# Keys of the first pair first, projection by halves, and a last image on two chains: a vision-transformer layer with a scheduling program inside

## The chip, the cores and the metric

The kernel runs on one core of one Trainium2 chip. The metric is the device time of one execution in microseconds (us), lower is better. All times below are of the kernel before the change.

## The reference, cut to what matters

Sixteen images of 3 x 512 x 512 are cut into 16 x 16 patches (1024 tokens of 768 numbers each), and pass a tokenizer and one layer of attention and feed-forward, all in float32:

```
h = patches(x) @ W.T + b                                  # 1024 tokens x 256 per image
q, k, v = split(layernorm(h) @ w_qkv)                     # 8 heads of 32
k = sum_{f=1..256} kan_a[f]*sin(f*k) + kan_b[f]*cos(f*k)  # elementwise on the keys
h = h + softmax(q k^T / sqrt(32)) v @ w_out + b_out
y = layernorm(h)
h = h + shared_mlp(y) + sum over the best 2 of 4 experts of weight_e * expert_e(y)
```

The sum over 256 frequencies for each key element (the "KAN" step) costs as much as the attention. The shared network has layers 256-256-128-256, each expert 256-128-64-256; the gate is a softmax over 4 experts, the best two are weighted by a second softmax.

## The kernel before, in words

**The work.** For an image, the 256 key rows are four "pairs" of heads. The KAN step works in groups `g` of eight key rows, eight groups a pair, 32 an image. A group has three tiles of 128 x 1024 integers: two "slow" waves, loaded from DRAM with copies along the partitions (`load_waves`, L871, tiles `w`), and one "fast" wave that VectorE spreads from a small source tile (`load_source` L890, `spread_waves` L911, tile `f`). GpSimd multiplies each by its frequency (`turn_waves`, L926), ScalarE takes the sine (`sine`, L936), TensorE mixes the two slow waves with the coefficients in tiles of 64 x 32 of the array (`mix`, L960), VectorE multiplies by the fast wave (`times_fast`, L974) and TensorE sums in tiles of 128 x 32 (`add_up`, L993). The finished keys of a pair go to DRAM and back in the order in which the scores need them (`finish_keys` L1012, `stack_keys` L1022). Attention runs once for each pair and each half of the queries, 128 times in all: scores (`score`, L1058, whole array), exponential on ScalarE (`exponential`, L1073), weighting of the values (`weigh`, L1090, tiles of 128 x 64), and a division (`normalize`, L1116 to L1135).

**Rounds.** The program is laid out in 130 rounds (at its end, `for rd in range(B * RI + 2)`). Round `rd` holds four KAN groups and attention number `att = rd - 2`: the first two rounds have no attention, the last two no KAN. On TensorE a round is a *KAN stretch* (four `mix`, then the first half of the sum) and then an *attention stretch* (eight score blocks, the second half of the sum, eight weightings). ScalarE takes the twelve sines of a round, then its eight exponentials, with a table switch before each kind.

**Pieces.** Everything else is put between as "pieces", written as Python generators that yield the engine that they need next and for how long: tokens (`tokens`), layer norms (`first_norm`, `transposed_layernorm`, tiles `hn`, `lnT`, `hnT`, `hT`), `keys`, `queries`, `values`, the projection (`project`), the gate (`gates`, `gate_weights`), and the feed-forward networks (`networks`). They are strung on four chains: 0 has keys, queries and values, 1 has projection, gates and networks, 2 the gate weights, 3 tokens and first norms. A chain goes on in its own order. Two PSUM banks (`side0`, `side1`) serve all pieces.

**What sets the order.** `run` is a planner that runs while the program is built. It keeps a clock for each engine, from costs written in the code, and lays down at each step the instruction that can start first: an item of a fixed queue (`put`, with a cost and dependencies), or the next piece of a chain. For TensorE it weighs a change of tiling (`SWITCH`, `retile`, `together`), and how much a chain is owed: each fixed TensorE item adds `pace * cost` to a chain's `due`, up to `most`, by the table `PACES` (one pair for each chain, L57); a laid piece takes its duration off again (L316), counted by `now["stream"]`, the streamed columns at `PER_COLUMN`. What the planner lays is the order that each engine then executes. Its clock is no measurement; engines wait for each other on the chip with semaphores.

**Places that the change touches.** `keys(b, rows)` makes 128 of the 256 key rows in two blocks of 512 tokens: two products (L263), about 4.2 us of range reduction on VectorE (L531 to L542), an addition on GpSimd (L544), and two stores to the DRAM tile `ud` from SP's queue (L546). The KAN groups of pairs 0 and 1 read rows 0 to 127 (`rows_of`: both blocks). At the start chain 1 holds `first_norm(0, 0), keys(0, 1)` and chain 0 `first_norm(0, 1), keys(0, 0)`. `project(b)` waits for the image's last attention (its "norm") and then does both halves of the tokens. `gates` and `networks` hold named locks (`gates`, `networks`, `s1`, `bands`), since their tiles exist once; for the very last half they run on chain 0 rather than 1, and keep the transposed norm in a part of `hnT`. The row `w5` of weights and the tiles `s1`, `s2`, `e1`, `e2` are shared by all halves.

Of the kernel before, what the change touches and what calls it, by code (L numbers as in the profile page):

```python
# [11 lines left out]
FP = mybir.dt.float32  # L12
# [6 lines left out]
P = 128  # L19
E = 256  # L20
NPAIR = 4
# [34 lines left out]
LAG, LANDS, TABLE, PER_COLUMN, SWITCH, IDLE = 0.06, 2.0, 1.28, 1.0 / 600, 0.18, 0.3  # L56
PACES = ((0.17, 2), (0.48, 3), (0, 0), (0.18, 2))  # L57

# [3 lines left out]
def plain_path(ctx: ExitStack, tc: tile.TileContext, a: dict, out: bass.AP, verdict: bass.AP):  # L62
# [140 lines left out]
    hnT = const.tile([P, 2, N], FP, tag="hnT", name="hnT")  # L203
    hT = const.tile([P, 2, 512], FP, tag="hT", name="hT")

    w5 = const.tile([NW5, 512], FPR, tag="w5", name="w5")
    bands = const.tile([P, 4, 4, NE + 1], FPR, tag="bands", name="bands")
# [13 lines left out]
    ]  # L221
    now = {"chain": 0, "stream": 0, "table": None, "dma": 0.0, "tiling": None}
    free = [0.0, 0.0]
# [63 lines left out]
    def step(c):  # L287

        ch = chains[c]
        now["chain"] = c  # L290
        bank, ch["bank"] = ch["bank"], None
        need = ch["need"]
        before = now["stream"]
        on = need[0] if isinstance(need, tuple) and need[0] in clock else None
        if on:
            at = max(clock[on], ch["ready"] + LAG)
            if on == PE:
                at = max(at, banks(c)[0][0] + LAG)
            ch["ready"] = clock[on] = at + (need[1] or 0.0)
            if bank is not None:  # L300
                free[bank] = ch["ready"]
        elif isinstance(need, tuple):
            ch["ready"] = max(ch["ready"], done[need])
        while True:
            if ch["gen"] is None:
                if not ch["gens"]:
                    ch["need"] = None
                    break
                ch["gen"] = ch["gens"].pop(0)
            try:  # L310
                ch["need"] = next(ch["gen"])
                break
            except StopIteration:
                ch["gen"] = None
        if on == PE:
            took = PER_COLUMN * (now["stream"] - before) + retile(None)  # L316
            ch["due"] -= took
            ch["ready"] = clock[PE] = at + took
# [117 lines left out]

    def transposed_layernorm(h, dst):

        yield from hold("s1")
        st = smp.tile([P, 4, 6], FP, tag="st", name="st")  # L440
# [11 lines left out]
        nc.gpsimd.tensor_tensor(less, less, rstd, ALU.mult)  # L452
        hn = ffp.tile([P, 4, E], FP, tag="s1", name="hn")
        for t in range(4):
# [5 lines left out]
        for c in range(2):  # L460
# [5 lines left out]
            nc.scalar.copy(dst[:, c, :], ps)  # L466
        locks.remove("s1")

# [37 lines left out]

    def keys(b, rows):

# [4 lines left out]
        if "ud" not in st:  # L513
            st["ud"] = udp.tile([E, 2, 2, N], INT, tag="ud", name="ud")
        for blk in range(2):
            yield "hnT", b, blk
# [164 lines left out]

    def project(b):

        yield "norm", 2 * NPAIR * (b + 1) - 1
        st = images[b]
        for half in range(2):
            h = st["h", half]
            for pr in range(2):
                yield GO
                ps = side_tile("proj").rearrange("p (t e) -> p t e", e=E)  # L690
                for t in range(2):
                    for c in range(2):
                        matmul(
                            out=ps[:, t, :],
                            lhsT=aT[:, c, ts(4 * half + 2 * pr + t, P)],
                            rhs=wo[:, c, :],
                            start=(c == 0),
                            stop=(c == 1),
                        )
                yield DVE, 0.63  # L700
                hh = h[:, ds(2 * pr, 2), :]
                nc.vector.tensor_add(hh, ps, hh)
            mark("projected", b, half)

    def gates(b, half, hT):
        yield "projected", b, half
        yield from hold("gates")
        yield from transposed_layernorm(images[b]["h", half], hT)
        yield GO
        ps = side_tile("gate")[:, 0:P]  # L710
        for c in range(2):
            for t in range(4):
# [6 lines left out]
                )  # L719
        now["stream"] += 3 * P  # L720
        yield ACT, 0.25
# [16 lines left out]

    def networks(b, half, hT):

        yield from hold("networks")

# [12 lines left out]
        def first_of_expert(e):  # L755
            yield GO
            ps = hidden(lambda c: w1e[:, 2 * e + c, :], "e1p")
            yield ACT, 0.6
            e1 = ff2.tile([P, 512], FP, tag="e1", name="e1")
            nc.scalar.activation(e1, ps, AF.Relu, bias=b1e[:, e : e + 1])  # L760
            return e1

        def second_of_experts(u, e1):
            yield GO
            ps = side_tile("e2p")
            for s in range(2):
                matmul(
                    out=ps[ts(s, 64), :],
                    lhsT=w2e[:, 2 * u + s, :],
                    rhs=e1[s],  # L770
                    start=True,
                    stop=True,
                )
            yield ACT, 0.6
            t = ff2.tile([P, 512], FP, tag="e2", name="e2")
            nc.scalar.activation(t, ps, AF.Relu, bias=b2e[:, u : u + 1])
            return t

        def weigh_experts(u, t):
            yield GO  # L780
            wb = side_tile("wb")
            matmul(out=wb, lhsT=sel[:, u, :], rhs=w5, start=True, stop=True)
            yield DVE, 0.63
            nc.vector.tensor_mul(t, wb, t)  # L784

        yield from hold("s1")
        s1 = ffp.tile([P, 2, 512], FP, tag="s1", name="s1")
        for m in range(2):
# [7 lines left out]
        for c in range(2):  # L796
# [6 lines left out]
            )  # L803
        locks.remove("s1")
        yield ACT, 0.6
        s2 = ffp.tile([P, 512], FP, tag="s2", name="s2")
        nc.scalar.activation(s2, ps, AF.Relu, bias=b2s)
# [40 lines left out]
        done["written", b, half] = sent(1.6, 0.5)  # L848
        locks.remove("networks")

# [27 lines left out]
    def load_source(p):  # L878
# [21 lines left out]

        deps = rows_of(8 * p) + ([("spread", 8 * p - 1)] if p > 0 else [])
        for j in range(2):
# [203 lines left out]
    def normalize(att):  # L1106
# [14 lines left out]
        def divide(s):  # L1121
# [8 lines left out]
            if i == 0 and b > 0:  # L1130
                deps.append(("projected", b - 1, 1))
            put(DVE, "norm", 0.69, deps, ("divide", att, s), action)
# [829 lines left out]
```

## Time and profile before

| what | value |
|---|---|
| median of 3 runs | 4232.87 us (4228.08 to 4237.59) |
| the profiled execution, own time | 4243.32 us |
| its span in the profile | 4241.8 us |
| PE, busy | 4058.3 us (96%) |
| ACT, busy | 3290.4 us (78%) |
| POOL, busy | 3195.6 us (75%) |
| DVE, busy | 2837.9 us (67%) |
| mean granted TensorE clock | 0.987 |
| moved by DMA | 914.27 MB, mean 216 GB/s |

The profiled execution took 4243.32 us, 10.45 us more than the median of the runs; its span is 1.5 us shorter than its own time. In the profile PE is TensorE, PEld its weight loads, ACT ScalarE, DVE VectorE, POOL GpSimd, SP the engine that issues most DMAs. A line such as `sT<-q,k` says that tile `sT` was written from `q` and `k`; "x4" that four instructions are merged; a bracket at the end is the idle time of the engine before it and what ended that. A float32 product on TensorE appears as two instructions. "Busy" of PE is not full use: an instruction that has started and waits for data counts.

### The profile page before, as it was taken

To read this page: it belongs to the slowest core of one execution; us is meant where nothing else is said; L and a number is where in the kernel's file an instruction comes from. 1 tells how busy PE (TensorE), PEld (TensorE's weight loads), DVE (VectorE), ACT (ScalarE), POOL (GpSimd) and SP (SyncE) were. 2 spreads that over 40 slices of the span, in tenths; PEclk is the share of its full clock that TensorE was granted. 3 is DMA by queue.
4 is the path that set the end of the run, shared out by engine and by line. 5 is a ranking of instruction groups with operands and counts; after the bars stand their busy time and mean duration, and the time that the engine had idled before them with its cause. 6 is when DMAs were issued, how large, how long until landed. Compare 5 with 4: busy or idle time off the path is not lost.

```text
span 4241.8 us, 67578 instructions
## 1 busy us (share of the span) xinstructions
PE 4058.3 (96%) x22753; PEld 1784.1 (42%) x22753; DVE 2837.9 (67%) x4172; ACT 3290.4 (78%) x3939; POOL 3195.6 (75%) x2323
## 2 busy tenths in 40 slices
PE   6889999999999999999999999999999999999997
PEld 4324344444444434444444444444444444443334
DVE  3666766767676675766767767676766767667652
ACT  1587888878888787887878878887888878788782
POOL 2888877787787787787778777877787778787750
PEclk9899999999999999999999999999999999999999
DMA  6988877878878887777878778787887978878750
GB/s 196 257 223 224 230 215 209 247 219 224 234 211 223 224 242 193 230 220 213 245 203 239 210 193 251 215 252 203 233 232 207 256 207 213 240 204 242 189 138 16
DMA packets 587479, 914.27 MB, mean 216 GB/s; under 512 B 58828, under 2 KB 177524, under 8 KB 587124
## 3 DMA queue, kind: packets, MB, share of 16 engines
q1 hardware_dynamic: 580880, 906.98, 77.8%
q8 instruction: 184, 3.01, 0.3%
q10 hardware_dynamic: 6244, 2.88, 0.3%
q14 instruction: 171, 1.40, 0.1%
HBM read 758.64 MB, written 150.99 MB: 214 GB/s over the span
## 4 chain that ended last, share of the span: by engine, by line
PE 59%; ACT 14%; DVE 8%; DMA 8%; issue 4%; SPq 3%; POOL 2%; ACTq 0%; DVEq 0%; POOLq 0%
PE av L1090 15%; PE sT L1058 10%; PE kan L960 6%; ACT w L936 6%; PE tok L263 5%; PE red L993 4%; PE e3p L263 4%; PE e1p L263 3%; ACT f L936 3%; DMA w<-ud 3%; DVE f L974 2%; PE k L263 2%; DMA q<-qd 2%; PE s1p L263 2%; PE proj L263 2%
## 5 line engine op out<-in xcount | busy, mean ns | idle before, releaser
L926 POOL TENSOR_TENSOR w<-w,lane 128x1024 int32<-128x1024 int32 x1024 | 1926.2, 1897 | 533.5 <-DMA w<-ud 289.1
L1073 ACT ACTIVATE es<-sT 128x1024 f32<-128x1024 f32 x1024 | 1033.5, 1023 | 583.0 <-PE av L1090 293.1
L926 POOL TENSOR_TENSOR f<-f,lane 128x1024 int32<-128x1024 int32 x512 | 971.0, 1896 | 193.5 <-DVE f L911 140.0
L936 ACT ACTIVATE w<-w 128x1024 f32<-128x1024 int32 x1024 | 1018.9, 1050 | 37.6 <-POOL w L926 36.2
L1090 PE MATMUL av<-es,v 128*64 128x512 f32 x4096 | 972.2, 605 | 2.3 <-ACT es L1073 2.1
L1116 DVE RECIPROCAL rc<-av 128x256 f32<-128x256 f32 x256 | 434.4, 1731 | 664.2 <-PE av L1090 664.1
L974 DVE TENSOR_TENSOR f<-kan,f 128x1024 f32<-128x1024 f32 x512 | 607.1, 1218 | 208.7 <-ACT f L936 161.6
L1058 PE MATMUL sT<-q,k 128*128 128x512 f32 x2048 | 686.8, 448 | 60.0 <-DVE f L974 26.9
L960 PE MATMUL kan<-w,coef 64*32 64x512 f32 x8192 | 641.4, 603 | 50.4 <-ACT w L936 42.4
L911 DVE STREAM_SHUFFLE f<-src 128x1024 int32<-128x1024 int32 x512 | 673.9, 1354 | 0.7
L1058 PEld LDWEIGHTS sT<-q,k 128*128 128x128 f32 x2048 | 351.7, 190 | 419.1 <-issue 179.3
L936 ACT ACTIVATE f<-f 128x1024 f32<-128x1024 int32 x512 | 512.9, 1052 | 0.0
L1090 PEld LDWEIGHTS av<-es,v 128*64 128x64 f32 x4096 | 260.5, 137 | 568.9 <-issue 499.8
L263 PE MATMUL tok<-wt,x 128*128 128x256 f32 x1536 | 366.9, 390 | 19.6 <-DMA w1s<-in_sW 13.4
L263 PEld LDWEIGHTS tok<-wt,x 128*128 128x128 f32 x1536 | 293.6, 194 | 108.7 <-issue 37.6
L960 PEld LDWEIGHTS kan<-w,coef 64*32 64x32 f32 x8192 | 135.3, 105 | 425.3 <-ACT w L936 248.1
L993 PE MATMUL red<-f,pack 128*32 128x512 f32 x2048 | 272.3, 604 | 0.0
L263 PE MATMUL e1p<-hT,w1e 128*128 128x512 f32 x496 | 242.0, 610 | 4.2 <-DVE e L784 3.8
L457 ACT ACTIVATE hn<-h,less,rstd 128x256 f32<-128x256 f32 x256 | 140.8, 592 | 81.4 <-POOL less L452 81.4
L1123 DVE TENSOR_TENSOR aT<-av,rc 32x512 f32<-32x512 f32 x256 | 176.1, 688 | 6.4
L936 ACT ACT_TABLE_LOAD x128 | 164.2, 1283 | 6.7 <-DMA w<-ud 4.4
L1200 ACT ACT_TABLE_LOAD x128 | 164.2, 1283 | 2.1
(125 smaller groups left out, 3742.2 us busy)
## 6 DMA issues: line engine op xcount, KB each, us to landing
w<-ud SPq DMA_DIRECT2D x2048, 256.0 KB
q<-qd SPq DMA_DIRECT2D x512, 128.0 KB
k<-kd SPq DMA_DIRECT2D x128, 512.0 KB
x<-in_xT SPq DMA_DIRECT2D x128, 384.0 KB
ud<-u SPq DMA_DIRECT2D x64, 512.0 KB
ud<-ui SPq DMA_DIRECT2D x64, 512.0 KB
src<-ud SPq DMA_DIRECT2D x512, 64.0 KB
qd<-qhi SPq DMA_DIRECT2D x64, 256.0 KB
```

Source lines behind the costliest of these rows:

```text
L263: nc.tensor.matmul(out=out, lhsT=lhsT, rhs=rhs, start=start, stop=stop)
L911: nc.vector.stream_shuffle(w, sources[g // 8].rearrange("p r n -> p (r n)"), [4 * (g % 8) + i // 8 for i in range(32)],)
L926: nc.gpsimd.tensor_tensor(w, w, f.to_broadcast([P, N]), ALU.mult)
L936: nc.scalar.activation(x, w, AF.Sin, scale=TURN * 2.0**-32)
L960: nc.tensor.matmul(out=ps[ds(64 * j + 32 * blk, 32), ts(r, 512)], lhsT=coef[ts(r, 64)].rearrange("p e f j -> p (e f j)"), rhs=w[ts(r, 64), ...
L974: nc.vector.tensor_mul(w, kan.pop(g), w)
L993: nc.tensor.matmul(out=rows_of_pair[p][ts(2 * i + r, 32), :], lhsT=pack[:, ds(PACK0 - 16 * (k % 2) - 2 * (k // 2), 32)], rhs=prod[:, ts(r, ...
L1058: nc.tensor.matmul(out=ps[:, ts(s, 512)], lhsT=k4[:, 2 * s + kc // 4, ts(kc % 4, P)], rhs=q4[:, s, :], start=True, stop=True,)
L1073: nc.scalar.activation(es, scores.pop(kc), AF.Exp, scale=SCALE)
L1090: nc.tensor.matmul(out=acc[0][ts(s, 64), :], lhsT=v[:, kc, p % NPAIR, ds(HD * s, 64)], rhs=es[:, ts(s, 512)], start=(kc == 0), stop=(kc == ...
L1116: nc.vector.reciprocal(rc[0][:, part], acc[0][:, part])
L1123: nc.vector.tensor_mul(aT[ds(64 * (i % 2) + HD * s, HD), i // 2, ts(qb, 512)], acc[0][ds(96 * s, HD), :], rc[0][ds(HD + HD * s, HD), :],)
```

## The change

- **Keys of the first pair's rows first.** `keys` takes the blocks to do. Chain 1 does block 0 of rows 0 to 127 after its norm, chain 0 block 1 after its own; only then chain 0 does rows 128 to 255. The first source tile waits until the first two wave tiles have been issued.
- **Projection by half.** `project(b, half)` waits for the last attention of its half only. The division of the next image's first attention waits for the projection of the same half, not of the second. Every half is followed on its chain as before by the gates and networks.
- **Last image.** Its half 0 stays on chain 1, its half 1 (projection, gates, networks) goes to chain 0. Both keep the transposed norm in their own half of `hnT`, take all working tiles from the pool of the wave tiles (`late_tile`, tag `w`, eight buffers), take `w5` from the pool of `f` tiles, and don't use the locks `s1` and `networks`. They wait until the last wave tile has been loaded. The lock `gates` stays.
- **Durations and shares.** `PACES` changes for three chains. A piece may name its tiling (`now["piece"]`), so that the gate counts like the sums and the experts' second layer like the weighting of the values; the gate counts 2P columns rather than 3P, the second layer 512 fewer, the weights' product 300 fewer.

No arithmetic is changed. The diff, cut to its core:

```
-PACES = ((0.17, 2), (0.48, 3), (0, 0), (0.18, 2))
+PACES = ((0.155, 2), (0.44, 2), (0, 0), (0.178, 2.6))
...
         if on == PE:
-            took = PER_COLUMN * (now["stream"] - before) + retile(None)
+            took = PER_COLUMN * (now["stream"] - before) + retile(now["piece"])
+            now["piece"] = None
...
-    def transposed_layernorm(h, dst):
+    def transposed_layernorm(h, dst, late=False):
...
-        yield from hold("s1")
+        if not late:
+            yield from hold("s1")
...
-        hn = ffp.tile([P, 4, E], FP, tag="s1", name="hn")
+        if late:
+            hn = late_tile(N, "hn").rearrange("p (t e) -> p t e", e=E)
+        else:
+            hn = ffp.tile([P, 4, E], FP, tag="s1", name="hn")
...
-    def keys(b, rows):
+    def keys(b, rows, blks=(0, 1)):
...
-        for blk in range(2):
+        for blk in blks:
...
-    def project(b):
+    def project(b, half):
...
-        yield "norm", 2 * NPAIR * (b + 1) - 1
-        st = images[b]
-        for half in range(2):
-            h = st["h", half]
+        yield "norm", 2 * NPAIR * (b + 1) - 2 + half
+        h = images[b]["h", half]
...
+    def late_tile(n, name):
+        return wp.tile([P, N], FP, tag="w", name=name)[:, 0:n]
...
-    def gates(b, half, hT):
+    def gates(b, half, late=False):
         yield "projected", b, half
+        if late:
+            yield "load", total - 1, 1
+            hT = images[b]["hT", half] = hnT[:, :, ts(half, 512)]
+        else:
+            hT = images[b]["hT", half] = hT_
         yield from hold("gates")
...
-        now["stream"] += 3 * P
+        now["stream"] += 2 * P
+        now["piece"] = TILINGS["red"]
...
+        w5 = fp.tile([P, 1024], FPR, tag="f", name="w5")[0:NW5, 0:512] if late else w5_
+        def room(pool, n, name):
+            return late_tile(n, name) if late else pool.tile([P, n], FP, tag=name[:2], name=name)
...
             ps = side_tile("e2p")
+            now["piece"] = TILINGS["av"]
+            now["stream"] -= 512
...
             wb = side_tile("wb")
+            now["stream"] -= 300
...
-        deps = rows_of(8 * p) + ([("spread", 8 * p - 1)] if p > 0 else [])
+        deps = rows_of(8 * p) + [("spread", 8 * p - 1) if p > 0 else ("load", 0, 1)]
...
-                deps.append(("projected", b - 1, 1))
+                deps.append(("projected", b - 1, qb))
...
-    feed(1, first_norm(0, 0), keys(0, 1))
+    feed(1, first_norm(0, 0), keys(0, 0, [0]))
+    feed(0, first_norm(0, 1), keys(0, 0, [1]))
     for b in range(B):
-        feed(0, *([first_norm(0, 1), keys(0, 0)] if b == 0 else [keys(b, 0), keys(b, 1)]))
+        feed(0, *([keys(b, 0)] if b else []), keys(b, 1))
...
-        feed(1, project(b))
+        late = b == B - 1
         for half in range(2):
-            late = half and b == B - 1
-            dst = hnT[:, :, 0:512] if late else hT
-            feed(1 - late, gates(b, half, dst), networks(b, half, dst))
+            feed(1 - (late and half), project(b, half))
+            if late:
+                feed(1 - half, gates(b, half, True), networks(b, half, True))
+        for half in range(2):
+            if not late:
+                feed(1, gates(b, half), networks(b, half))
```

The order of instructions that the planner lays can be read from the built programs without running them; the prediction uses such counts.

More of the change, by code (lines that the diff above doesn't have):

```diff
@@ L203, in plain_path @@
     hnT = const.tile([P, 2, N], FP, tag="hnT", name="hnT")
-    hT = const.tile([P, 2, 512], FP, tag="hT", name="hT")
-    w5 = const.tile([NW5, 512], FPR, tag="w5", name="w5")
+    hT_ = const.tile([P, 2, 512], FP, tag="hT", name="hT")
+    w5_ = const.tile([NW5, 512], FPR, tag="w5", name="w5")
     bands = const.tile([P, 4, 4, NE + 1], FPR, tag="bands", name="bands")
@@ L221, in plain_path @@
     ]
-    now = {"chain": 0, "stream": 0, "table": None, "dma": 0.0, "tiling": None}
+    now = {"chain": 0, "stream": 0, "table": None, "dma": 0.0, "tiling": None, "piece": None}
     free = [0.0, 0.0]
@@ L466, in transposed_layernorm @@
             nc.scalar.copy(dst[:, c, :], ps)
-        locks.remove("s1")
+        if not late:
+            locks.remove("s1")
     def tokens(b, half):
@@ L680, in gate_weights @@
         locks.remove("bands")
-    def project(b):
-        yield "norm", 2 * NPAIR * (b + 1) - 1
-        st = images[b]
-        for half in range(2):
-            h = st["h", half]
[L688 to L703, printed above, removed]
-    def gates(b, half, hT):
-        yield "projected", b, half
+    def project(b, half):
+        yield "norm", 2 * NPAIR * (b + 1) - 2 + half
+        h = images[b]["h", half]
+        for pr in range(2):
+            yield GO
+            ps = side_tile("proj").rearrange("p (t e) -> p t e", e=E)
+            for t in range(2):
+                for c in range(2):
+                    matmul(
+                        out=ps[:, t, :],
+                        lhsT=aT[:, c, ts(4 * half + 2 * pr + t, P)],
+                        rhs=wo[:, c, :],
+                        start=(c == 0),
+                        stop=(c == 1),
+                    )
+            yield DVE, 0.63
+            hh = h[:, ds(2 * pr, 2), :]
+            nc.vector.tensor_add(hh, ps, hh)
+        mark("projected", b, half)
+    def late_tile(n, name):
+        return wp.tile([P, N], FP, tag="w", name=name)[:, 0:n]
+    def gates(b, half, late=False):
+        yield "projected", b, half
+        if late:
[3 more added lines that the diff above has]
+            hT = images[b]["hT", half] = hT_
         yield from hold("gates")
-        yield from transposed_layernorm(images[b]["h", half], hT)
+        yield from transposed_layernorm(images[b]["h", half], hT, late)
         yield GO
@@ L737, in rest, with networks @@
         yield from gen
-    def networks(b, half, hT):
-        yield from hold("networks")
+    def networks(b, half, late=False):
+        if not late:
+            yield from hold("networks")
+        hT = images[b]["hT", half]
+        w5 = fp.tile([P, 1024], FPR, tag="f", name="w5")[0:NW5, 0:512] if late else w5_
+        def room(pool, n, name):
+            return late_tile(n, name) if late else pool.tile([P, n], FP, tag=name[:2], name=name)
         def hidden(lhsT, name):
@@ L758, in first_of_expert @@
             yield ACT, 0.6
-            e1 = ff2.tile([P, 512], FP, tag="e1", name="e1")
+            e1 = room(ff2, 512, "e1")
             nc.scalar.activation(e1, ps, AF.Relu, bias=b1e[:, e : e + 1])
@@ L774, in second_of_experts @@
             yield ACT, 0.6
-            t = ff2.tile([P, 512], FP, tag="e2", name="e2")
+            t = room(ff2, 512, "e2")
             nc.scalar.activation(t, ps, AF.Relu, bias=b2e[:, u : u + 1])
@@ L784, in weigh_experts @@
             nc.vector.tensor_mul(t, wb, t)
-        yield from hold("s1")
-        s1 = ffp.tile([P, 2, 512], FP, tag="s1", name="s1")
+        if not late:
+            yield from hold("s1")
+        s1 = room(ffp, 1024, "s1").rearrange("p (m n) -> p m n", m=2)
         for m in range(2):
@@ L803, in networks @@
             )
-        locks.remove("s1")
+        if not late:
+            locks.remove("s1")
         yield ACT, 0.6
-        s2 = ffp.tile([P, 512], FP, tag="s2", name="s2")
+        s2 = room(ffp, 512, "s2")
         nc.scalar.activation(s2, ps, AF.Relu, bias=b2s)
@@ L848, in networks @@
         done["written", b, half] = sent(1.6, 0.5)
-        locks.remove("networks")
+        if not late:
+            locks.remove("networks")
     total = B * NG
@@ L1164, in plain_path @@
                 feed(3, first_norm(b, half))
-        feed(1, project(b))
+        late = b == B - 1
         for half in range(2):
-            late = half and b == B - 1
-            dst = hnT[:, :, 0:512] if late else hT
-            feed(1 - late, gates(b, half, dst), networks(b, half, dst))
+            feed(1 - (late and half), project(b, half))
+            if late:
+                feed(1 - half, gates(b, half, True), networks(b, half, True))
+        for half in range(2):
+            if not late:
+                feed(1, gates(b, half), networks(b, half))
     for g in range(total):
```

## The prediction, made before the changed kernel ran

> **What bounds the kernel now.** First the page's slices, then busy time by stretch, then the timeline at start, middle and end.
>
> ```profile
> PE   6889999999999999999999999999999999999997
> ACT  1587888878888787887878878887888878788782
> PEclk9899999999999999999999999999999999999999
> ```
>
> TensorE is the bound in all but the first three slices and the last one, 106 us each. Where it isn't full:
>
> ```profile
> 70.00:105.00 35.00, 20.95 (x72) 10.58 (x76) 13.73 (x26) 9.72 (x21) 12.65 (x12) 0.77 0.82 257
> 105.00:140.00 35.00, 30.68 (x158) 13.71 (x152) 19.96 (x32) 22.33 (x26) 32.62 (x22) 0.84 1.06 259
> 140.00:175.00 35.00, 29.64 (x159) 13.41 (x158) 25.66 (x38) 16.06 (x17) 30.14 (x19) 0.91 0.94 274
> 4150.00:4175.00 25.00, 16.80 (x64) 9.79 (x63) 10.45 (x20) 5.58 (x8) 1.72 (x4) 0.85 0.00 0
> ```
>
> Columns: length; busy PE, PEld, DVE, ACT, POOL with counts; granted clock; DMA share; GB/s. From 105 on GpSimd is the full engine of the start (32.62 of 35), and the DMA engines are near theirs. The start:
>
> ```profile
> 52.71 12.52 SPq L431 DMA_DIRECT2D x<-in_xT  x2
> 65.28 0.54 SPq L546 DMA_DIRECT2D ud<-u  x1
> 73.63 0.42 SPq L546 DMA_DIRECT2D ud<-ui  x1
> 88.19 11.44 SPq L871 DMA_DIRECT2D w<-ud  x16
> ...
> 93.07 1.90 POOL L926 TENSOR_TENSOR w<-w,lane 128x1024 int32<-128x1024 int32 x1 [19.92 <-issue]
> ...
> 186.49 3.78 PE L263 MATMUL q<-hnT,wq 128*128 128x512 f32 x4 [4.81 <-DVE qlo L559]
> 189.28 2.29 PE L1058 MATMUL sT<-q,k 128*128 128x512 f32 x4
> ```
>
> Pair 0's last keys are stored at 73.63, but SP has query stores and eight source copies ahead of the first wave (88.19); GpSimd's first turn is at 93.07, the first attention at 189.28. A round with no pieces:
>
> ```profile
> 231.49 3.90 PE L960 MATMUL kan<-w,coef 64*32 64x512 f32 x32 [0.98 <-ACT w L936]
> 237.17 3.90 PE L960 MATMUL kan<-w,coef 64*32 64x512 f32 x32 [1.78 <-ACT w L936]
> 241.01 1.06 PE L993 MATMUL red<-f,pack 128*32 128x512 f32 x8
> ```
>
> KAN stretch (kan's start to the first score, 242.22) 10.73 us, in which TensorE has 4.27 us to stream and waits for sines; attention stretch 15.31; together 26.04. The end:
>
> ```profile
> 4156.58 3.72 PE L263 MATMUL proj<-wo,aT 128*128 128x256 f32 x16
> 4162.89 5.41 PE L263 MATMUL proj<-wo,aT 128*128 128x256 f32 x16 [2.58 <-DVE h L702]
> 4173.88 2.80 PE L267 MATMUL lnT<-ident,hn 128*128 128x128 f32 x8 [5.59 <-ACT hn L457]
> ```
>
> After the last weighting the norm of half 0 waits for the projection of both halves (statistics end at 4171.15); from 4178.8 to 4233.3 TensorE is idle for only about 5 us.
>
> **What the Trainium skill says.** "TensorEngine Tiling (Array Packing)", Key Properties: changing the tiling mode drains TensorE. The trace agrees: by starts of consecutive blocks, a change costs 0.16 us (av to whole array), 0.17 (kan to whole), 0.20 (whole to kan), 0.14 (red to av), over what the columns stream. "DMA: Bandwidth & Descriptors", Anatomy of one DMA: a semaphore wait is made on the issuing sequencer before dispatch, so what stands behind waits too. The trace agrees: the two x loads held SP for 12.52 us, while `ui` was done at 61.35 and its store went at 65.28. The same section gives about 2.0 us of fixed cost per DMA; the `ud` store here delays its reader by 3.7 us, which I use. "TensorE: Matmul & The Clock Gate", What's actually happening: half clock after idling; the windows show 0.77 and 0.85.
>
> **Part 1, the start.** In the new order the product for rows 0-127, block 1 follows two token tiles directly. Tokens at 49.92, two of 2.7: 55.3; product 1.7: 57.0; range reduction 0.69+0.70+1.42+0.68+0.69 = 4.2 and 0.3 for the bank: 61.5; GpSimd 1.04, store 0.9: 63.6, before 74.05. SP then issues the first wave at once: 3.7 for the store: 67.3. Issue to turn took 4.9 (88.19 to 93.07): first turn 72.2 instead of 93.07. But the first fast wave needs eight source copies (0.7 each, 5.6), behind six wave copies (4.3) and with two pairs of `ud` stores (1.8): 79.0; landing 2.0, spread 1.35, turn 1.9: 84.3, before 99.4. So 15.1 earlier.
>
> From there to the last turn of group 11 GpSimd took 80.9 us before: 33 turns x 1.853 = 61.1, two norms 3.5, two `h` additions 4.7, four `u` 4.1, stalls 7.5. New order: two `u` fewer (-2.0), a copy of `v` more (0.7), stalls taken equal: 79.6, so 163.9 instead of 180.3. The first score stood 9.0 us behind, 4.81 of that a wait of the queries for VectorE. In the new order a sum and one token tile stand there, no query: about 4.5. First score 168.4, that is 20.9 earlier. Its attention stretch holds another token tile: round 1 begins at 168.4 + 15.3 + 2.7 = 186.4, before 205.4: 19.0 earlier.
>
> What was not done by then: counting products ahead of the first score, one token tile, two key products and eight of queries fewer: 2.56 + 1.71 + 6.83 = 11.1 us. Of these 8.5 lie in rounds 1 and 2, 1.7 in an attention stretch (paid), 6.8 in KAN stretches with 6.4 us free each (I take 1.0). The remaining token tile was counted. Gain 19.0 - 2.7 = **16 us**. The cover is the 26.04 us round; without it the gain is 10. Both ends: 4 (DMA, rival C) and 20 (no stalls).
>
> **Part 2, the middle.** I laid the planner's order against the trace, round by round. Work is the same, 217 us of streaming in eight rounds. Over the program, tiling changes go from 1767 to 1832, and in rounds 1-125 the pieces in the KAN stretches grow by 69 us, those in the attention stretches shrink by 59 (10 come from the start). Attention stretches of before fit 11.95 + pieces + 0.2 for each change: paid in full. A KAN stretch is the larger of 4.27 + pieces + 0.19 a change, and what ScalarE needs for its sines and the pieces' evictions: 10.7 with none, 12 to 13.6 measured with few pieces. With that floor at 12, 12.5, 13 and 13.5, rounds 12-125 add up to 3466, 3481, 3500, 3522 before, and 3476, 3487, 3501, 3522 after: +10, +6, +1, 0. Thus moving pieces beside the sines gains little, since most KAN stretches are full already (round 24 of before: 11.94 of pieces, 17.15 measured, 17.16 by the sum). I take **+4 us**; ends -30 and +38 (rivals B, D). `PACES` and the named tilings act only through this order.
>
> The measured stretches exceed my sum by some 120 us; nearly all of this is latency in particular rounds, which an order changes one way or the other.
>
> The looser wait of the division, half against half, removes a wait that no long idle row shows: 0. It stands in VectorE's queue with the next division behind it; if its cover went, at most one projection product, 1.7 us, would show.
>
> **Part 3, the end.** TensorE's order still has the projections after the last weighting, because chain 1 finishes the networks of image 14 only just before. But VectorE's order now has the additions of half 0 between the reciprocals, divisions and check, and its statistics before the last additions of half 1. From the last reciprocal (4160.1): one addition 0.69, two divisions 1.39, check 0.77, addition 0.69, then four statistics of 0.55 with two additions of 0.69 between and about 1 us of waiting: 4168.2 at the latest, at best 4166, instead of 4171.15. So -3 to -5, and 0 to -2 from the gaps that half 1's first layer fills. The eight shared late buffers can make half 1 wait for half 0's third layer: 0 to +2. **-5 us**, ends -1 and -7.
>
> **Sum.** -16 + 4 - 5 = -17 against the profiled execution: 4243.3 - 17 = 4226. The runs' median is 10.45 lower; taking the difference over, 4232.9 - 17 = **4216**.
>
> **Rivals.** A, as above: 4216, chance 0.50.
>
> B, stalls go as well: in rounds 40, 48, 56, 64, 72 the attention stretch took 21.8, 23.6, 20.3, 21.1, 23.7, in rounds 80 and 88 with the same pieces 16.2: 29.7 us too many in all. There SP's wave copies last 16.6 us instead of 12.3, GpSimd's norm comes late, and exponentials queue behind it on ScalarE. Those rounds have two token tiles and four projections; the new order has no such round repeated. For it: five stalls of one pattern. Against: tokens are as many, and may meet loads elsewhere. 25 of 30 gone: 4191, chance 0.17.
>
> C, the start gives nothing back: 1.06 and 0.94 of the DMA engines were busy from 105 to 175; the same waves in less time may wait for them, which the 1.9 and 2.9 us stalls of GpSimd hint at. Gain 4 instead of 16: 4228, chance 0.16.
>
> D, slower: pieces now split the `mix` blocks oftener, and each split exposes a sine or an eviction. A fit of before's KAN stretches gives 0.59 us for each change, not 0.19. 65 x 0.59 = +38, with nothing gained by the move: 38 - 21 = +17, 4250. It decides from 0.45 us a change upward. For it: kan to red exceeds its columns by 0.57 us on average, kan to whole by 0.43. Against: that mean has sine waits that pieces may fill. Chance 0.17.
>
> **Range and chances.** A difference of 0.2%, 8.5 us, is about what a measurement of this kernel can tell from none. A is beyond it in five of six (0.42 faster, 0.07 same, 0.01 slower), B is faster, C mostly same (0.13, 0.02 faster, 0.01 slower), D slower but for 0.02. Faster 0.61, same 0.22, slower 0.17. The range takes in B and C whole and D up to 4248: 4188 to 4248.
>
> **What would show it.** First turn near 72, first score near 168 (C: beyond 180). Rounds 1 and 2 near 29 and 27 us. Rounds 12-125 at 31.6 us on average (B: 31.4 or less; D: 31.9 or more), KAN stretches longer and attention stretches shorter. After the last weighting 73 us to the last product instead of 77. The prediction is wrong if GpSimd's stalls in the start grow by over 8 us, or rounds of the middle change by over 0.1 us each.

## The result, and the profile after

| | median of the runs | span of the profiled execution | PE busy | mean granted clock |
|---|---|---|---|---|
| before | 4234.15 us (4228.08 to 4237.59) | 4241.8 us | 4058.3 us | 0.987 |
| after | 4171.03 us (4169.02 to 4171.34) | 4169.3 us | 4027.4 us | 0.993 |

The ratio of after to before is 0.9851, with a 95% interval of 0.9834 to 0.9869: 63 us faster, where the prediction had 17. The sign was right, the time lies below the range. The two profiles are 72.5 us apart; before's profiled execution was 9 us above its runs' median, after's lies on it, so the parts below, read from profiles, add up to more than 63.

The busy slices of after's page, for comparison with those of before:

```profile
PE   6889999999999999999999999999999999999998
ACT  2688888788787888878788888788788788888873
PEclk9999999999999999999999999999999999999999
```

They look alike; the page at this width doesn't show where 63 us went. Next come the same stretches of the start as before, and 25 us around the end of the last weighting at 4086.6 (length; busy PE, PEld, DVE, ACT, POOL; clock; DMA share; GB/s):

```profile
70.00:105.00 35.00, 24.27 (x118) 9.12 (x116) 17.47 (x30) 16.68 (x26) 25.54 (x20) 0.90 0.96 303
105.00:140.00 35.00, 26.44 (x160) 12.97 (x160) 20.44 (x35) 21.70 (x26) 32.81 (x18) 0.90 0.93 255
140.00:175.00 35.00, 32.40 (x158) 16.50 (x158) 22.20 (x33) 20.67 (x24) 31.98 (x22) 0.90 1.08 280
4078.00:4103.00 25.00, 20.30 (x94) 10.54 (x90) 9.89 (x20) 8.37 (x11) 1.71 (x4) 0.91 0.04 12
```

GpSimd is busy for 25.5 us in the first of them, before for 12.7, with the DMA engines at 0.96 rather than 0.82: the waves come earlier. The start in after's timeline:

```profile
61.64 0.46 SPq L552 DMA_DIRECT2D ud<-ui  x1
62.20 4.38 SPq L898 DMA_DIRECT2D w<-ud  x2
...
69.67 1.90 POOL L953 TENSOR_TENSOR w<-w,lane 128x1024 int32<-128x1024 int32 x1 [4.04 <-DVE ui L548]
83.60 1.90 POOL L953 TENSOR_TENSOR f<-f,lane 128x1024 int32<-128x1024 int32 x1 [7.31 <-DVE f L938]
...
164.07 1.28 PE L1085 MATMUL sT<-q,k 128*128 128x512 f32 x4
```

The first wave is issued at 62.20 (88.19 before), the first turn is at 69.67 (93.07), the first score at 164.07 (189.28). Rounds are counted here, as in the prediction, by the number of their attention, from 0; the loop variable `rd` is larger by 2. Round 1 begins 26.1 us earlier, round 3 by 23.6. At round 126 the lead is 71.3 us, so the middle gave some 48; the rest of the program adds 1. The middle can't be read from long idle rows. So TensorE's timeline of rounds 16 to 103 (eleven images of eight rounds) is cut at the first score of each round and behind its last weighting, and the table has the mean of an image. "Excess" is what a stretch took above the prediction's sums (4.27 + pieces + 0.19 a tiling change for KAN, 11.95 + pieces + 0.2 for attention). The two kernels between are experiments told below:

```
                              image us  KAN us  attention  KAN excess  att. excess
before                          254.6    115.7    138.9       8.5         2.6
before + new start              253.3    116.0    137.4       8.4         1.5
after, projection as a whole    252.3    115.9    136.4       9.5        -1.4
after                           250.4    119.4    131.0       5.9         0.5
```

Pieces moved from attention to KAN stretches as the prediction said, and the excess fell from 11.1 us an image to 6.4, which it had not said.

### The profile page after: what moved, and what is told of

It is laid out like the page before. It is cut to its first block, busy times and chain, and to the rows that moved or that the text cites. A ratio compares the mean times of both kernels' runs of the same rounds, so it can differ in the third digit from the quotient of the medians.

```text
span 4169.3 us, 67564 instructions
## 1 busy us (share of the span) xinstructions
PE 4027.4 (97%) x22753; PEld 1766.4 (42%) x22753; DVE 2830.2 (68%) x4172; ACT 3286.3 (79%) x3939; POOL 3195.8 (77%) x2323
## 4 chain that ended last, share of the span: by engine, by line
PE 74%; ACT 10%; DVE 6%; DMA 5%; issue 3%; SPq 2%; POOL 1%; ACTq 0%; DVEq 0%; POOLq 0%
PE av L1117 18%; PE sT L1085 11%; PE kan L987 9%; PE tok L263 6%; PE e3p L263 5%; PE red L1020 5%; PE e1p L263 5%; ACT w L963 4%; DMA w<-ud 3%; PE s1p L263 3%; PE q L263 2%; PE v L263 2%; PE proj L263 2%; DVE f L1001 2%; PE k L263 2%
## 5 line engine op out<-in xcount | busy, mean ns | idle before, releaser
L987 PE MATMUL kan<-w,coef 64*32 64x512 f32 x8192 | 623.9, 600 | 39.5 <-ACT w L963 35.6
L263 PE MATMUL e1p<-hT,w1e 128*128 128x512 f32 x480 | 233.2, 608 | 0.4 <-ACT e L799 0.4
```

The source lines that it names most:

```text
L263: nc.tensor.matmul(out=out, lhsT=lhsT, rhs=rhs, start=start, stop=stop)
L987: nc.tensor.matmul(out=ps[ds(64 * j + 32 * blk, 32), ts(r, 512)], lhsT=coef[ts(r, 64)].rearrange("p e f j -> p (e f j)"), rhs=w[ts(r, 64), ...
```

## The experiments

**1. The parts, each alone.** Before with the new start alone (the hunks on `keys`, `load_source` and the first two `feed`), with shares and durations alone, and with the waits by half alone:

```
 first:   deps = rows_of(8 * p) + [("spread", 8 * p - 1) if p > 0 else ("load", 0, 1)]   and the new feeds
 second:  PACES, now["piece"], now["stream"] of the change
 third:   project(b, half), deps.append(("projected", b - 1, qb))
```

> Before, with the first part of the change alone (keys of rows 0-127 first, on two chains; the first source tile after the first two wave tiles). Pieces and their places in rounds 12 to 125 stay almost as before (17 us of streaming in other stretches, against 350 for the whole change). Theory (the start is worth 24 us and the stalls of the middle come from the order of pieces in an image): 4234 - 24 = 4210 us, round 3 begins near 234, and rounds 40, 48, 56, 64, 72 still stall by 3 to 7 us each. Rival (the stalls depend on where loads fall against the rounds, and the earlier start alone moves them away): 4185 us or less, no such stalls.

> Before, with PACES and the durations and tilings of the pieces as changed, all waits and the start as before. If the planner's shares and durations carry the middle: 4234 - 45 = 4189 us. If the waits by half carry it: 4234 within 8 us. If each of the 50 more tiling changes costs 0.5 us: 4259 us.

> Before, with the projection by half and the division that waits for the same half alone. If the waits by half carry the middle: 4234 - 45 = 4189 us. If shares and durations carry it: 4234 within 8 us. The order of the pieces changes here too (313 us of streaming in other stretches), so a third case is that any new order loses the five stalls: 4234 - 25 = 4209 us.

New start: 4208.06 us, ratio to before 0.9945 (0.9929 to 0.9962), 26 us faster. Its round 3 begins at 236.0, and rounds 48, 56, 64, 72 stall by 5.2, 4.1, 3.0 and 4.4 us: the first theory. Shares and durations: 4223.42, 0.9975 (0.9964 to 0.9985), 11 us faster, which is none of the three cases; the stalls of rounds 40 to 72 are gone, but other KAN stretches grew. Waits by half: 4265.67, 1.0073 (1.0056 to 1.0090), *slower* by 31, which no theory had. One place decides it: 15 us ahead of before at round 45, it is 27 behind at round 49, and the KAN stretch of round 46 between them is 17.8 us above the sum.

**2. The whole change without one part.** After with the old `PACES`, without the new start, and with the last image in the old rooms and on the old chains:

```
 first:   PACES = ((0.17, 2), (0.48, 3), (0, 0), (0.18, 2))
 second:  feed(1, first_norm(0, 0), keys(0, 1)) ...   as before
 third:   feed(1, project(b, 0), project(b, 1)); gates and networks of the last image without late rooms
```

> After, with the old PACES alone. If the shares carry the middle: 4171 + 45 = 4216 us. If durations or waits by half carry it: 4171 within 8 us. If the middle is a matter of which order happens to avoid stalls: anywhere between, with stalls over 3 us in named rounds that make up the difference.

> After, with the start as before (rows 128-255 on chain 0 with the first norm, the source tile not held back). If the start adds 26 us to whatever the middle does: 4171 + 26 = 4197 us. If the gain of the middle hangs on when the start ends: 4215 us or more, with stalls in the middle that after does not have.

> After, with the last image on the old rooms, locks and chains (only its half 1 apart on chain 0). The order of rounds 1 to 125 is the same as after's. By the two profiles the new end is worth 2.3 us: 4173 us. By the prediction 5 us: 4176 us. If the lower clock of the end is what the two chains bring: 4171 or less.

Old `PACES`: 4339.23 us, ratio to before 1.0256 (1.0238 to 1.0273). It is 168 us slower than after for three pairs of numbers, where 45 were expected. Without the new start: 4206.42, 0.9932 (0.9916 to 0.9949), so the start is worth 35 us here and 26 on before; some 9 us depend on how the order falls afterwards. Old end: 4170.51, 0.9846 (0.9829 to 0.9862): separate rooms and two chains are worth nothing that can be measured.

Where most of the 168 us lie shows round 46 with the old `PACES`. TensorE, then GpSimd, then VectorE, in that kernel's timeline:

```profile
1616.70 1.06 PE L987 MATMUL kan<-w,coef 64*32 64x512 f32 x8 [0.79 <-ACT w L963]
1627.35 3.78 PE L263 MATMUL e1p<-hT,w1e 128*128 128x512 f32 x4 [9.59 <-DVE qlo L565]
...
1587.25 1.04 POOL L550 TENSOR_TENSOR u<-ui,quarter 128x512 int32<-128x512 int32 x1 [4.44 <-DVE ui L548]
1599.29 1.90 POOL L953 TENSOR_TENSOR w<-w,lane 128x1024 int32<-128x1024 int32 x1 [11.00 <-DMA w<-ud]
...
1625.88 0.69 DVE L564 CAST qhi<-q 128x512 fp32r<-128x512 f32 x1 [11.16 <-DMA ud<-ui]
```

And what SP's queue waited for from 1560 to 1632 (total, times, longest):

```profile
SPq L552 <- POOL rank L671: 17.9, 1, 17.9
SPq L1066 <- PE sT L1085: 6.1, 1, 6.1
```

SP stands 17.9 us at a store of keys (L552), whose `u` GpSimd has not yet made because the key product came late; the wave copies of the next image stand behind it, and GpSimd has no wave to turn for 11.00 us. TensorE's one long wait comes later and is not for a sine. VectorE stands 11.16 us before it splits queries (`qhi`, `qlo`), until a store of keys (`ud<-ui`), issued late as well (1616.99), has landed: the split takes its tiles from the same rooms as `u` and `ui` (tags `u` and `r`). TensorE's `e1p` stands 9.59 us until `qlo` is done. The same pair is in all seven stretches named next (TensorE 7.6 to 9.6 us, VectorE 8.9 to 11.2). The Trainium skill ("DMA: Bandwidth & Descriptors", Anatomy of one DMA) says that a wait for a semaphore is made on the issuing sequencer before dispatch; the trace agrees, and shows that what stands behind waits too: 17.9 us. KAN stretches of rounds 38, 46, 54, 62, 70, 78 and 86 exceed the sum by 13.3 to 16.1 us. For the image that begins at round 40, TensorE's order has the four key products of the next image in rounds 40 + 2, 5, 5 and 5; in after they lie in rounds 40 + 0, 2, 3 and 4.

**3. Are late keys the stall?** After with chain 1's old pair alone; with all old `PACES` but a larger share for chain 0, so that keys come early; and with chain 0's old share alone:

```
 first:   PACES = ((0.155, 2), (0.48, 3), (0, 0), (0.178, 2.6))
 second:  PACES = ((0.25, 2), (0.48, 3), (0, 0), (0.18, 2))
 third:   PACES = ((0.17, 2), (0.44, 2), (0, 0), (0.178, 2.6))
```

> After, with the old pair of chain 1 alone, (0.48, 3). In TensorE's order the last key product of an image then lies in the seventh of its eight rounds (8b + 6), in after in the fifth (8b + 4). If late keys are what stalls (the experiment with all old PACES had its last key product in the sixth round, and stalls of 15 us in rounds 38 to 86): 13 images by 15 us or more, 4171 + 195 = 4366 us. If the old pair only fills the stretches otherwise: the sum over rounds 12 to 125 with a KAN stretch of at least 13.5 us is 9 us less than after's: 4162 us.

> The experiment with all old PACES (4339 us), with chain 0's share 0.25 in place of 0.17, so that the last key product of an image comes in the third round (8b + 2) and not in the sixth. Chain 1's pair stays (0.48, 3). If late keys are what stalls: no stalls of 15 us, and 9 us less than after by the same sum: 4162 us, 4150 to 4190. If the old pair of chain 1 or the waits by half stall for another reason: 4300 us or more.

> After, with the old share of chain 0 alone, 0.17. Keys come earlier (last product in the third round). The sum over rounds 12 to 125 with a KAN stretch of at least 13.5 us, tilings at 0.19 us, is 3501 us against 3522 for after: 4171 - 21 = 4150 us. If that sum says nothing of the time, or keys at the fifth round were early enough and nothing else counts: 4171 within 8 us.

Chain 1's pair: 4267.82 us, 1.0078 (1.0062 to 1.0095): 97 us slower than after, not 195. No stretch has a stall of 15 us; the loss shows as stalls of 4.6 and 5.2 us in two KAN stretches of an image, and 2.7 in an attention stretch. So the *last* key product isn't what counts. Early keys: 4192.56, 0.9901 (0.9884 to 0.9917): one number took 147 of the 168 us away, and round 46's KAN stretch from 35.74 us to 16.43. Late keys were the stall; 4192.56 is 30 us above the 4162 expected, so the rest of the order counts too. Chain 0's old share: 4210.56, 0.9949 (0.9932 to 0.9965), 39 us slower than after where the sum with a floor of 13.5 us had said 21 faster. That sum doesn't rank orders.

The product that the failed expectation pointed to is the second: rows 0 to 127, both blocks, feed the first two pairs of the next image, rows 128 to 255 only the last two. Say that an image begins at round 8b. With chain 1's old pair the second key product of the next image lies in round 8b + 4, with all old pairs in 8b + 5 for just the images that stall, and with the waits by half alone in 8b + 6 for just the image that begins at round 40. An exception is the image that begins at round 16: with that product in round 21, two kernels lost only 3 us in round 22. An order with the second product in 8b + 6 for three images tests it:

```
 PACES = ((0.155, 2), (0.45, 2), (0, 0), (0.175, 2.6))
```

> After, with chain 1's pair (0.45, 2) and chain 3's (0.175, 2.6). The second key product of images 10, 12 and 14 falls into round 8b + 6 (b counted from the image before: rounds 78, 94, 110), in the others into 8b + 2. If that product's place makes the stall: KAN stretches 15 us too long in rounds 78, 94 and 110 and in no other of that kind; 4171 + 28 (the sum with the floor of 13.5 us) + 45 = 4244 us. If it is the last product or the whole order: no such three stalls, and 4199 us by the sum.

4257.8 us, 1.0055 (1.0033 to 1.0077). The KAN stretches of rounds 78, 94 and 110 exceed the sum by 7.0, 7.0 and 7.8 us, and of the others with over 7 us of pieces none by over 2. They last 56.7, 56.7 and 57.5 us, since the planner's own clock saw the gap and put 44 us of pieces there; the timeline of round 78 has no mix for its first 42 us:

```profile
2557.02 0.66 PE L267 MATMUL lnT<-ident,hn 128*128 128x128 f32 x4
...
2570.77 1.88 PE L263 MATMUL k<-hnT,wk 128*128 128x512 f32 x4
...
2599.55 1.95 PE L987 MATMUL kan<-w,coef 64*32 64x512 f32 x32
2601.43 1.98 PE L263 MATMUL q<-hnT,wq 128*128 128x512 f32 x4
```

Against after, the program falls back by 42.5 us there and gets 10 to 15 back in the next rounds, since those pieces are done. From round 77 on, the three times 16 rounds with such a product lose 27, 31 and 34 us, where 15 each, and 28 in all for the rest of the order, were expected. The places were right, the size was not.

**4. Durations, and which wait by half.** After with the old durations and tilings; with both waits set back (the projection of all images but the last as a whole), then each of the two alone:

```
 first:   retile(None); now["stream"] += 3 * P; no now["piece"], no corrections for e2p and wb
 second:  yield "norm", 2 * NPAIR * (b + 1) - 1     (b < B - 1)   and   deps.append(("projected", b - 1, 1))
 third:   only the latter (division)
 fourth:  only the former (projection)
```

> After, with the old durations and tilings of the pieces (new PACES). The sum as above is 3558 us, 36 more than after's, and the last key product lies in the sixth round's first half (8b + 5). If keys there are early enough: 4171 + 36 = 4207 us. If they are too late: 4300 us or more. If durations don't matter: 4171 within 8 us.

> After, with the projection of every image but the last waiting for both halves again, and the division for the projection of half 1. The new PACES stay. If new shares alone make the middle faster: 4171 within 8 us. If waits by half and new shares are needed together (each alone moved the middle by -11 and +31 us): the middle of the second experiment with the new start, 4234 - 26 - 11 - 2 = 4195 us or more.

> After, with the division of an image's first attention waiting for the projection of half 1 again, as before. TensorE's pieces lie in the same stretches as after's. If the projection's wait carries the 22 us: 4171 within 8 us. If the division's does: 4193 us.

> After, with the projection waiting for both halves again (but in the last image), the division for its own half. TensorE's pieces lie in the same stretches as with both waits set back: the first KAN stretch of an image has 4.3 us of pieces, not 7.5. If the projection's wait carries the 22 us: 4193 within 8 us. If the division's does: 4171 us.

Old durations: 4302.07 us, 1.0156 (1.0136 to 1.0176), 131 us slower than after, with second key products in 8b + 3 and 8b + 4 and stalls of 2 to 6 us in many rounds. The case "too late" fits better than "early enough", though 8b + 4 was not late enough for one long stall. Both waits back: 4193.52, 0.9902 (0.9885 to 0.9918), as expected. Division's wait back alone: 4169.60, 0.9847 (0.9826 to 0.9868), so it is worth nothing. Projection's wait back alone: 4194.76, 0.9903 (0.9881 to 0.9924). So it is the projection's wait, 23 us, in this order of pieces. On before's order the two waits by half cost 31, and one changed share (chain 0's above, chain 3's below) costs 39 and 30; that 23 us are the price of the wait, and not of any new order, rests on the stretches that follow.

How a wait that no idle row shows can be worth 23 us: the KAN stretch of round 48, the first of an image. With the projection as a whole, timeline of the fourth kernel:

```profile
1626.52 2.86 PE L263 MATMUL tok<-wt,x 128*128 128x256 f32 x12
1629.31 2.16 PE L987 MATMUL kan<-w,coef 64*32 64x512 f32 x32
1633.25 3.90 PE L987 MATMUL kan<-w,coef 64*32 64x512 f32 x32 [1.78 <-ACT w L963]
1637.09 1.99 PE L263 MATMUL proj<-wo,aT 128*128 128x256 f32 x8
1639.01 1.06 PE L1020 MATMUL red<-f,pack 128*32 128x512 f32 x8
```

and in after:

```profile
1623.70 1.99 PE L263 MATMUL proj<-wo,aT 128*128 128x256 f32 x8
1625.53 0.60 PE L267 MATMUL lnT<-ident,hn 128*128 128x128 f32 x4
1626.06 1.09 PE L987 MATMUL kan<-w,coef 64*32 64x512 f32 x16
...
1627.81 1.99 PE L263 MATMUL proj<-wo,aT 128*128 128x256 f32 x8
1629.64 1.88 PE L263 MATMUL k<-hnT,wk 128*128 128x512 f32 x4
1631.45 1.95 PE L987 MATMUL kan<-w,coef 64*32 64x512 f32 x32
1633.33 1.99 PE L263 MATMUL proj<-wo,aT 128*128 128x256 f32 x8
```

The mix counts as busy while it waits for sines inside (3.90 us for 2.16), so half the loss is no idle time in the profile. The two stretches, fourth kernel and after, by engine:

```profile
1626.52:1640.01 13.49, 11.71 (x95) 5.00 (x93) 13.09 (x20) 13.00 (x15) 9.49 (x11) 1.00 1.06 245
```

```profile
1623.70:1637.27 13.57, 13.53 (x110) 6.93 (x109) 13.21 (x16) 13.55 (x15) 11.27 (x8) 1.00 0.86 220
```

Both last 13.5 us, for ScalarE is busy for 13.00 and 13.55 of them; VectorE is as full (13.09 and 13.21), so either may set the length, though the wait inside the stretch was for a sine. After does 7.7 us of pieces in that time, the other 4.3: the projection of half 0 may start with the image's last attention but one, so that there is something to lay beside the sines. In the mean of eleven images, the first two KAN stretches exceed the sum by 7.5 us with the whole projection and 2.1 with halves; part of that comes back as excess elsewhere, and the image is 1.8 us shorter, 26 us in the 114 rounds of the middle. Before, whose projection also waits for both halves, exceeds the sum in these two stretches by 3.3 us only: most of the gap that the halves fill came with the new shares.

**5. What stalled in rounds 48 to 72.** The kernel of the first experiment with the norm's four small steps on VectorE:

```
-        nc.gpsimd.tensor_scalar(rstd, mv[:, :, 1], EPS, None, ALU.add)
-        nc.gpsimd.tensor_tensor(rstd, rstd, mhalf, ALU.pow)
+        nc.vector.tensor_scalar(rstd, mv[:, :, 1], -0.5, 1.5, ALU.mult, ALU.add)
...
+        nc.vector.tensor_scalar(less, mv[:, :, 0], -1.0, None, ALU.mult)
+        nc.vector.tensor_tensor(less, less, rstd, ALU.mult)
```

> The first experiment's kernel (before with the new start) with the four small steps of each norm moved from GpSimd to VectorE, where a straight line 1.5 - x/2 stands in for the power -1/2, so the output differs. TensorE's order is the same to the instruction. If late wave copies hold GpSimd, the norm waits behind them, and exponentials wait behind the norm on ScalarE: the attention stretches of rounds 48, 56, 64 and 72 lose their stalls of 5.2, 4.1, 3.0, 4.4 us: 4208 - 17 = 4191 us. If the late waves themselves are what TensorE waits for: 4208 within 5 us, with the stalls moved to the sines of the next stretch.

In the first experiment's timeline, round 48 (GpSimd, then ScalarE):

```profile
1641.30 1.90 POOL L926 TENSOR_TENSOR w<-w,lane 128x1024 int32<-128x1024 int32 x1 [9.70 <-DMA w<-ud]
1645.11 1.90 POOL L926 TENSOR_TENSOR w<-w,lane 128x1024 int32<-128x1024 int32 x1 [1.92 <-PE red L993]
1647.09 0.23 POOL L448 TENSOR_SCALAR rstd<-mv 128x4 f32<-128x4 f32 x1
...
1640.94 1.94 ACT L1073 ACTIVATE es<-sT 128x1024 f32<-128x1024 f32 x2 [2.25 <-PE sT L1058]
1649.07 0.60 ACT L457 ACTIVATE hn<-h,less,rstd 128x256 f32<-128x256 f32 x1 [6.19 <-POOL less L452]
```

and ScalarE with the norm on VectorE:

```profile
1655.27 1.94 ACT L1072 ACTIVATE es<-sT 128x1024 f32<-128x1024 f32 x2 [3.23 <-PE sT L1057]
1657.10 0.60 ACT L456 ACTIVATE hn<-h,less,rstd 128x256 f32<-128x256 f32 x1
```

The chain is as supposed: GpSimd waits 9.70 us for a late wave copy, the norm stands behind that, and ScalarE, in order, holds six exponentials behind the norm for 6.19 us. With the norm on VectorE these attention stretches lose their stall (round 48: 21.72 to 16.07 us) and 13 us are gained between rounds 45 and 73. Yet the time is 4209.86, 0.9943 (0.9926 to 0.9959), against 4208.06: 3.6 us were lost by round 1, another 10 up to round 45, and 6 from round 73 to 125, spread thinly, with the same order on TensorE; what stands behind round 125 is 6 us shorter. What the three steps hold up on VectorE was not traced. So the stall's mechanism is shown, and this way to remove it gains nothing.

**6. An order chosen by the sum.** After with chain 3's share 0.175:

> After, with chain 3's share 0.175 in place of 0.178. The pattern of after's rounds 20 to 61 then holds through the whole program. The sum with the floor of 13.5 us is 3504 us, 18 less than after's: 4153 us if the sum tells. In after itself an image took as long in rounds 20 to 61 as later: 4171 within 8 us if the pattern alone counts. The experiment with chain 0's old share was 39 us slower at 21 less by the sum: 4210 if that holds here too.

4201.24 us, 0.9919 (0.9897 to 0.9940): 30 us slower than after, where the sum had 18 faster; the last of the three cases, 4210, came nearest. The pattern of after's rounds 20 to 61 doesn't hold: from round 64 on a token tile moved by a round, and the attention stretches of rounds 65, 73, 81 and so on exceed the sum by 2.5 to 5.4 us, in which ScalarE does the four `hn` of a norm among the exponentials. Choosing `PACES` by this sum failed twice in two tries.

## Why the prediction was wrong

**What bounds the kernel** was read rightly, but too coarsely: in a KAN stretch such as round 48's with the whole projection, with 8.5 us to stream, the bound is not TensorE but ScalarE (13.00 of 13.49 us) or VectorE (13.09), and the slices can't show it.

**Part 1, the start: right in mechanism, -16 for -23.6.** First turn 69.7 (72.2 predicted), end of the first `f` turn 85.5 (84.3), first score 164.1 (168.4). The terms off: GpSimd's stalls up to group 11, taken equal at 7.5, were 2.2, and the attention stretch behind the first score took 15.3 us with its token tile, which was charged 2.7 more and was free. (A slip in its sum is small: 61.5 + 1.04 + 0.9 is 63.4, not 63.6.) The work left over cost 2.5 us by round 3 (26.1 less 23.6), as the 2.7 worked out. Rival C is refuted: at a DMA share of 0.93 to 1.08 the start gave nothing back.

**Part 2, the middle: this step failed.** It said that moving pieces gains little, +4, and that the 120 us by which the stretches exceed the sum are latency that an order changes "one way or the other", so none of it was counted. By the prediction's own terms, rounds 12 to 125: the sum rose by 15 us (3434 to 3450), as it should with 65 more tiling changes; the excess fell by 34 in KAN stretches (140 to 105) and by 26 in attention stretches (30 to 4). The floor of 13.5 us gave "0" and does: 3522 for both kernels. What lies above it fell from 82 to 37 us. Of the change's parts, on the new start, shares and durations gave 15 us (4208 to 4194; the five stalls of rival B among them), the projection's wait 23 us more (4194 to 4171), the division's nothing, as predicted. The projection by half was priced only through its order of pieces; that it fills the first KAN stretches of an image, which the sines make as long anyway, was missed. Rival B named the right stalls and, at 4191, came closest; it lacked the projection's 23. Rival D, dearer tiling changes, is refuted: 65 more went with a smaller excess.

**Part 3, the end: -2 for -5.** The statistics are complete 9.6 us after the projections begin, not 14.6: that 5 is as worked out. Of it 2.8 were lost behind, in two blocks at half clock. In windows of 0.5 us the granted clock is 0.50 for some 10 us around the transposes of half 0's norm: from 4170.9 to 4181.2 before, 4098.5 to 4108.7 in after, 4099.8 to 4110.0 with the old end. Half 0's first layer (`s1p`) began 2.4, 4.9 and 3.5 us before that ended, and took 4.78, 6.06 and 5.38 us; times its mean clock that is 3.6 in all three. After alone has a second such time, from 4118.9 to 4122.4, in which a layer of an expert took 3.45 us instead of 1.98. With the old rooms and chains the lead is 2 us smaller, and the end comes at the same time (after, then old end):

```profile
4098.86 2.80 PE L267 MATMUL lnT<-ident,hn 128*128 128x128 f32 x8 [3.46 <-ACT hn L462]
4103.75 6.06 PE L263 MATMUL s1p<-hnT,w1s 128*128 128x512 f32 x8
4119.38 3.45 PE L263 MATMUL e1p<-hnT,w1e 128*128 128x512 f32 x4 [0.18 <-ACT e L799]
4160.86 0.27 PE L1252 MATMUL okT<-ident,worst 128*1 128x128 f32 x1
```

```profile
4101.59 2.80 PE L267 MATMUL lnT<-ident,hn 128*128 128x128 f32 x8 [5.58 <-ACT hn L462]
4106.47 5.38 PE L263 MATMUL s1p<-hnT,w1s 128*128 128x512 f32 x8
4121.40 1.99 PE L263 MATMUL e1p<-hnT,w1e 128*128 128x512 f32 x4 [0.24 <-ACT e L799]
4161.33 0.27 PE L1248 MATMUL okT<-ident,worst 128*1 128x128 f32 x1
```

From the first projection (4086.56 and 4087.17) the last product stands 74.3 and 74.2 us away, before 76.5. The same layer before, and the clock in these blocks (same columns as above; before, then after twice):

```profile
4178.77 4.78 PE L263 MATMUL s1p<-hnT,w1s 128*128 128x512 f32 x8
4178.77:4183.55 4.78, 4.78 (x10) 2.12 (x10) 1.28 (x9) 0.90 (x2) 1.76 (x9) 0.75 0.00 0
```

```profile
4103.75:4109.81 6.06, 6.06 (x10) 2.56 (x10) 1.27 (x9) 0.90 (x2) 1.76 (x9) 0.59 0.00 0
4118.81:4122.83 4.02, 3.84 (x7) 1.70 (x8) 0.00 (x0) 1.01 (x2) 0.00 (x0) 0.58 0.00 0
```

**The sum.** 26 (start on before) + 15 + 23 + 0 = 64 of 63 us measured. These are steps of one path from before to after, so they must add up. On other paths the parts differ: the start is worth 35 on the changed middle, and the change without its durations (4302), without its shares (4339), and before with the halves alone (4266) are all slower than before.

**Open.** Why the order with the norm's steps on VectorE loses 19 us up to round 125; which of the many short stalls an order meets, short of running it; what makes up the 4 to 5 us stalls with chain 1's old pair; and whether new shares, chosen anew for a projection as a whole, would win back its 23 us.

## What to carry to other kernels

Where a planner works around a wait, its idle row alone doesn't give its price: ask which stretch, bound by another engine, could have been filled if the work had been free to start, and count that stretch's spare time. Where shares set an order, look first for the deadline of the pieces that feed a single in-order DMA queue (here the second key product, by the fifth of eight rounds): here an image that missed it lost 13 to 34 us, while short stalls in an order that kept it added up to 131 us in the program (the old durations). And don't take measured excess over a cost sum as constant under a new order: here it was the whole effect in the middle, and no static sum ranked the orders.

## What the runs showed of the hardware that was not expected

- Nothing but three pairs of planner numbers made 168 us (4%) on the same arithmetic; orders without a stall of 15 us lay anywhere between 4170 and 4302 us.
- A block of mixes that waits for sines inside counts as busy for 3.90 us instead of 2.16: its instructions start by eights every 0.95 us, at the pace of the sines (3.89 us for four). With the same products TensorE was "busy" for 4058 us before and 4027 after.
- In the tail the granted clock was 0.50 for some 10 us around a norm in three kernels. One layer took 4.78, 5.38 and 6.06 us in them, the longer the more of it lay in that time, so a part of what an earlier start gained was lost again (2.8 of 5 us, with a second such time).
- With three VectorE steps of a few elements in place of four on GpSimd for each norm, 19 us were lost up to round 125, while the removed stalls gave 13 and the tail 6: no gain.
